# A graph layer's gather and segment sum: 56 window quads and 423 gathered chunks in place of 64 and 352, stores by SyncE, the second sort beside the first quads, the loop unrolled

## The chip, the cores and the metric

The kernel runs on one core of one Trainium2 chip. Time is the device time of one execution in microseconds. The kernel before took 15,360.9 us, the median of three runs between 15,360.42 and 15,367.33.

A core has five engines with instruction queues of their own, each worked in order: TensorE (PE), VectorE (DVE), ScalarE (ACT), GpSimd (POOL) and SyncE (SP). SP, ACT and POOL can issue DMA transfers; an indirect transfer, which takes its row numbers from a table in the on-chip memory, is issued by POOL in this kernel.

## The reference

```
h = relu(layernorm(x))                       # x: 100000 x 64, float32
local, nbr = h[dst], h[src]                  # 3.3 million edges, sorted by dst
y = concat([local, nbr - local]) @ W.T + b
s = segment_sum(y, dst, 100000); cnt = segment_sum(1, dst)
out = x + where(cnt > 0, s / max(cnt, 1), 0)
```

As the layer is linear, the kernel sums the neighbours' rows h[src] for each node first, and multiplies the mean by W once per node. The heavy part is that segment sum: 3.3 million rows, picked by src, added up by dst. For precision each float32 row of h is kept as three bfloat16 parts side by side (table h3, 194 columns), so that one-hot matmuls add it exactly enough.

## The kernel before

It has four stages: a pre-stage (layer norm, the table h3 and the own part hb), a sort of the edges of the windows, the segment sum, and a post-stage (division, the matmul with W, the residual).

The edges, in order of dst, are split in two sets, which are summed in two ways at the same time.

**Quads.** The first 2,039,808 edges make 256 windows of 7968 edges; one window's dst numbers span fewer than CH = 256 nodes. Four windows make a quad, 64 quads in all. Each window's edges are sorted by src on DVE (`sort_lane`: a merge network on keys, 128 windows at once, one per partition; two such lanes). A step of the network copies one half of a piece of keys to `tmp`, a tile in PSUM, by ACT (line 455), and takes minimum and maximum by DVE (lines 456 and 457). At its end it counts where each block of 640 nodes begins (lines 533, 588). `fill_lane` then reads the sorted keys back, 32 or 64 of each window and block, by indirect transfers of POOL (kf, line 636, 161 per lane, and kx, line 721, 64 per lane for the edges left over), and writes small tables sr_d, dt_d, et_d and xs_d to DRAM by SP. `quads` streams the whole table h3, as 157 blocks of 640 nodes, through the core once per quad: SP loads three blocks at a time (tab, line 761, three buffers), with srs (line 752) and dt (line 756); DVE makes one-hots gh and dh, two blocks at a time (lines 789 and 340); PE picks rows by gh (line 811, into gp), ACT copies them (gs, line 813), and PE adds them by dh to the quad's sums (line 819, total). A quad has 158 such block steps (NE), 79 turns of the loop. At its end ACT copies total (line 835, 4 copies), DVE adds the own counts, and POOL adds each window's sums to acc in DRAM (line 849). Some edges of a quad that fit no slot are read by two indirect transfers (rows_x, line 778).

**Chunks.** The other edges make 352 chunks of 3584. `chunks` reads every edge's row by indirect transfers of POOL, 128 rows each, 28 per chunk (nb, line 391, 9856 in all), into 6 buffers of 14. DVE makes a one-hot of 14 x 128 x 128 (hot, line 340), PE adds up in PSUM (ps, line 396), DVE folds the three parts (sums, line 407), and POOL adds the 128 sums to acc (line 366, indirect, 58 chunks; line 371, a direct add at an address read from base_r, 294 chunks).

**What sets the order.** The program is written as generators that take turns. `gathers(ns)` gives out one gather of `chunks` for each GATHER = 1250 ns that the work beside it was reckoned to take, and `took` counts each fill transfer as one such. Lane 0 is sorted first, then lane 1 with lane 0's fill beside it; then four quads (U0) with lane 1's fill, all with gathers between; then a loop of three turns (`For_i`), each with 20 quads (SB) and 98 chunks (KB). `add_later` puts off the adds of a chunk or window by 56 gathers.

```
owed += 2 * (KB * J - 1) / (SB * NE)
while owed > 0:
    next(ev, None)
    owed -= 1
```

This is the loop's own pace: KB x J = 2744 gathers are spread evenly over a turn's 20 quads. At the end of the stage a test on `odd` decides whether a slow general path (lines 932 to 985) has to run; for these inputs it doesn't.

Of the kernel before, what the change touches and what calls it, by code (L numbers as in the profile page):

```python
# [32 lines left out]
LANES = 2  # L33
SB = 20
KB = 98
U0 = 4
KG = 16
# [3 lines left out]
STEP = 1050  # L41
GAP = 8
# [19 lines left out]
PIECE = 1536  # L62
COUNTS = 1
GAIN = 2.0 ** 40
PART = 1024
# [19 lines left out]
def plan(v, e):  # L85

    wl = 1 << int(np.log2(33 * CH * 1.05))
    ew = wl - PAD
    nw = LANES * P
    chunks = -(-(e - nw * ew) // CHUNK)  # L90
    return wl, nw, max(chunks, (nw // W - U0) // SB * KB)


@with_exitstack
def gnn_preln(ctx: ExitStack, tc, x, src_w, dst_w, src_p, dst_p, src_a, dst_a, wT, b, out, V, E):
# [27 lines left out]
    SETS = NL * G  # L123
# [7 lines left out]
    PA = NCH - (SETS - U0) // SB * KB  # L131
# [4 lines left out]
    assert 2 * C == P and NCB % 2 == 1 and PA >= 0 and SL % 2 == 0  # L136
# [9 lines left out]
    wb_d = dram.tile([SETS * W, 1], I32, name="wb_d")  # L146
# [28 lines left out]
    wb_r = consts.tile([1, SETS * W], I32, name="wb_r")  # L175
    turns = consts.tile([1, 2], I32, name="turns")
    ones = consts.tile([P, 1], F32, name="ones")
# [4 lines left out]
    odd = consts.tile([P, 1 + 5 * LANES], F32, name="odd")  # L182
# [22 lines left out]
    with tc.tile_pool(name="pre", bufs=2) as pre, tc.tile_pool(name="small", bufs=4) as small, \  # L205
# [32 lines left out]
        most = small.tile([P, NMT], F32, name="most", bufs=1)  # L238
        nc.vector.memset(least, 0.0)
        nc.vector.memset(most, 0.0)  # L240

        def bounds(m):
# [3 lines left out]
            nc.vector.tensor_reduce(least[:n, m:m + 1], d[:n], axis=AX.X, op=ALU.min)  # L246
            if m == NMT - 1:

                nc.vector.scalar_tensor_tensor(d[:n], d[:n], float(V), d[:n], op0=ALU.is_lt, op1=ALU.mult)
            nc.vector.tensor_reduce(most[:n, m:m + 1], d[:n], axis=AX.X, op=ALU.max)  # L250
            if m < NMT - 1:
                return
            span = small.tile([P, NMT], F32, name="span", bufs=1)
            nc.vector.tensor_sub(span, most, least)
            nc.vector.tensor_reduce(odd[:, 0:1], span, axis=AX.X, op=ALU.max)
            nc.vector.tensor_scalar(odd[:, 0:1], odd[:, 0:1], float(P), None, op0=ALU.is_ge)
# [55 lines left out]
    with tc.tile_pool(name="rows", bufs=6) as rows, \  # L312
# [5 lines left out]
        def number(at, engine, most):  # L318
            with tc.issue_after(last[engine].ins):
                return nc.values_load(at, engines=[engine], min_val=0, max_val=most)  # L320
# [5 lines left out]
        later = []  # L326
        count = [0, 0]
# [4 lines left out]
        def add_now(all_of_them=False):  # L332
            while later and (all_of_them or (later[0][0] <= count[0] and count[0] - count[1] >= GAP)):
                later.pop(0)[1]()
                count[1] = count[0]

# [8 lines left out]
        def chunks(first, n, dynamic=None):  # L345


            def load(q):
# [7 lines left out]
                nc.vector.tensor_sub(rel[:, :k], di[:, :k], base_b[:, at][:, :, None].to_broadcast([P, k, J]))  # L356
                near = index.tile([P, KG, J, D], I16, name="near")
                nc.vector.tensor_scalar(near[:, :k], rel[:, :k, :, None].to_broadcast([P, k, J, D]), float(2 * CH), None,
                                        op0=ALU.min)
                to = index.tile([P, KG], I32, name="to", bufs=3)  # L360
                nc.vector.tensor_scalar(to[:, :k], base_b[:, at], pcol, None, op0=ALU.add)
                return si, near, to

            def addition(q, rows_to, sums):
                if dynamic is None:
                    nc.gpsimd.indirect_dma_start(  # L366
                        out=acc, out_offset=bass.IndirectOffsetOnAxis(ap=rows_to, axis=0),
                        in_=sums, in_offset=None, compute_op=ALU.add)
                else:
                    at = number(base_r[0:1, ds(dynamic + q, 1)], POOL, V)  # L370
                    nc.gpsimd.dma_start(acc[ds(at, P)], sums, accum_op=ALU.add)  # L371

            ahead = load(0)
            before = None
            parts = J // JH
            for k in range(n * parts + 1):
                q, part = divmod(k, parts)
                u = q % KG
                if q < n:
                    if u == 0 and part == 0:  # L380
                        si, near, to = ahead
                    hot = rows.tile([P, JH, P], BF16, name="hot", bufs=4)
                    nb = rows.tile([P, JH, CT], BF16, name="nb")
                    with behind():
                        one_hot(hot, near[:, u, part * JH:part * JH + JH], P)
                if before is not None and before[2] == 0:
                    ps = rows_ps.tile([P, CE], F32, name="ps")
                for j in range(JH):
# [6 lines left out]
                    if before is not None:  # L395
                        nc.tensor.matmul(ps, lhsT=before[0][:, j], rhs=before[1][:, j, :CE],  # L396
# [7 lines left out]
                if before is not None and before[2] == parts - 1:  # L404
                    sums = rows.tile([P, C1], F32, name="sums", bufs=LAG + 2)
# [4 lines left out]
                    add_later((LAG - 1) * J, lambda b=before[3], s=sums: addition(*b, s))  # L410
                if q < n:
                    before = (hot, nb, part, (q, to[:, u:u + 1]))
# [5 lines left out]
        def sort_lane(l, keys, piece, few, ps):  # L418

            whole = keys.bitcast(I32)  # L420
# [3 lines left out]
            nc.vector.tensor_scalar_min(wb[:, 0:1], wb[:, 0:1], float(V - CH))  # L424
            last[DVE] = nc.vector.tensor_reduce(wb[:, 1:2], whole[:, :EW], axis=AX.X, op=ALU.max)
# [6 lines left out]
            mine = slice(l * P, l * P + P)  # L432
            for i in range(W):
                nc.sync.dma_start(wb_d[mine].rearrange("(g i) o -> i g o", i=W)[i], wb_i[i * G:i * G + G])
            nc.sync.dma_start(wb_r[:, mine], wb_d[mine].rearrange("w o -> o w"))
            for a in range(0, EW, PART):
# [12 lines left out]
                last[DVE] = nc.vector.scalar_tensor_tensor(d, d, 1, s[:, :n],  # L449
                                               op0=ALU.logical_shift_left, op1=ALU.bitwise_or)  # L450
# [3 lines left out]
            def exchange(lo, hi, tmp):  # L454
                last[ACT] = nc.scalar.copy(tmp, lo)  # L455
                nc.vector.tensor_tensor(lo, tmp, hi, ALU.min)  # L456
                last[DVE] = nc.vector.tensor_tensor(hi, tmp, hi, ALU.max)  # L457
# [601 lines left out]
```

## Time and profile before

| what | value | where it is from |
|---|---|---|
| median of the runs | 15,360.9 us | times |
| the profiled execution | 15,353.34 us, span 15,351.7 us | times, page |
| granted TensorE clock, mean | 0.889 | profile by cores |
| first and last gather (line 391) | 437.5 and 14,998.8 us | the tile nb |
| first fill of lane 0, of lane 1 (line 636) | 1568.1 and 2594.6 us | timeline of POOL |
| first gp matmul of the quads | 2575 us | timeline |
| HBM traffic | 267 GB/s over the span, some 310 in the loop | page |

The span is what the profiler saw from the first to the last instruction; the time has 1.6 us more. The page gives for each engine its busy time, which counts neither the waits nor the sequencer's own steps. A group's row has the line, the engine, the operation, the tile written and those read, how often, then its busy time, the mean of one in ns, and the idle time just before its instructions with what ended it; "issue" there is idle time in which the engine waited for nothing that the profile shows. Rows of a table by stretches give the length, the busy time of each engine with the number of its instructions, the granted clock, the share of time in which the DMA engines were busy, and GB/s. A pause on an engine that nobody waits for costs nothing.

### The profile page before, as it was taken

The page shows a single profiled execution, that of the slowest core. Times are in us where ns is not written, and L with a number is a line of the kernel's source. Part 1 is how long each engine was busy: PE and PEld are TensorE (multiplying, and loading weights), DVE is VectorE, ACT ScalarE, POOL GpSimd, SP SyncE. Part 2 cuts the span into 40 slices and gives each one's busy share as a digit, 9 for nine tenths or more (in the row PEclk, how much of TensorE's full clock was granted, in tenths as well). Part 3 has the DMA queues.
Part 4 walks back from the last instruction along what each step waited for, and adds up shares of the span by engine and source line. Part 5 has one row for each costly group of instructions (what it writes and reads, how often), then busy time and mean ns, then how long its engine had stood idle before and what let it go on. Part 6 is the DMA issues. An engine that isn't in the chain of part 4 may idle for free. (4 is left out here: it accounts for less than half of the span.)

```text
span 15351.7 us, 559362 instructions
## 1 busy us (share of the span) xinstructions
PE 11536.5 (75%) x238778; PEld 9464.2 (62%) x238778; DVE 11308.7 (74%) x15452; ACT 6104.8 (40%) x11710; POOL 11131.2 (73%) x11210
## 2 busy tenths in 40 slices
PE   6101001596998989998799999899879999989985
PEld 5100001475777777777677777777767777777775
DVE  6889797675777777777677777777767777777774
ACT  5335344342444444444344444444334444444441
POOL 4776766547777777777777777777777777777776
PEclk7555555798999999999899999999999999999997
DMA  7573233796999999999899999999989999999997
GB/s 295 124 106 55 48 52 80 189 318 213 313 314 309 318 306 309 307 312 306 264 309 321 311 318 307 304 311 315 299 268 314 319 309 312 313 307 310 311 302 281
DMA packets 1746424, 4097.89 MB, mean 267 GB/s; under 512 B 943899, under 2 KB 952230, under 8 KB 1738950
## 3 DMA queue, kind: packets, MB, share of 16 engines
q1 hardware_dynamic: 1182534, 3461.26, 64.6%
q0 software_dynamic: 454208, 535.92, 17.0%
q10 hardware_dynamic: 107168, 64.74, 2.1%
q8 instruction: 1877, 30.75, 0.8%
q14 instruction: 637, 5.22, 0.1%
HBM read 3880.72 MB, written 219.04 MB: 267 GB/s over the span
## 5 line engine op out<-in xcount | busy, mean ns | idle before, releaser
L391 POOL DMA_INDIRECT nb<-h,si x9856 | 9427.8, 957 | 3263.5 <-issue 2820.4
L813 ACT CAST gs<-gp 128x386 bf16<-128x386 f32 x10048 | 4830.0, 482 | 7085.4 <-PE gp L811 6870.8
L811 PE MATMUL gp<-tab,gh 128*128 128x193 bf16 x60288 | 6225.4, 251 | 978.0 <-DMA tab<-tables 590.5
L811 PEld LDWEIGHTS <-gh 128*128 128x128 bf16 x60288 | 4887.1, 99 | 1992.3 <-issue 923.2
L340 DVE TENSOR_TENSOR dh<-dt,c 128x1024 bf16<-128x1024 int16 x5056 | 3454.8, 683 | 2861.1 <-PE total L819 2728.8
L789 DVE TENSOR_TENSOR gh<-srs,c 128x1536 bf16<-128x1536 int16 x5056 | 4765.1, 942 | 19.0 <-PE gp L811 17.5
L819 PE MATMUL total<-gs,dh 32*128 32x193 bf16 x160768 | 4411.6, 247 | 40.8 <-issue 38.6
L819 PEld LDWEIGHTS <-dh 32*128 32x128 bf16 x160768 | 3193.2, 94 | 1073.2 <-issue 1054.1
L396 PE MATMUL ps<-nb,hot 128*128 128x193 bf16 x9856 | 1802.3, 263 | 2458.4 <-DVE sums L409 1862.0
L396 PEld LDWEIGHTS <-hot 128*128 128x128 bf16 x9856 | 972.4, 104 | 2417.1 <-DVE sums L409 1911.8
L455 ACT COPY tmp<-keys 128x1536 f32<-128x1536 f32 (+14 forms) x540 | 650.3, 1214 | 1226.6 <-DVE keys L457 1009.1
L456 DVE TENSOR_TENSOR keys<-tmp,keys 128x1536 f32<-128x1536 f32 (+14 forms) x540 | 757.1, 1423 | 80.3 <-ACT tmp L455 79.3
L340 DVE TENSOR_TENSOR hot<-near,c 128x1792 bf16<-128x1792 int16 x704 | 760.4, 1080 | 9.6 <-PE ps L396 9.5
L457 DVE TENSOR_TENSOR keys<-tmp,keys 128x1536 f32<-128x1536 f32 (+14 forms) x540 | 757.1, 1422 | 2.3
L849 POOL DMA_DIRECT2D acc<-wsums x256 | 347.6, 1358 | 191.8 <-DVE gh L789 67.3
L636 POOL DMA_INDIRECT kf<-ksort,at_i x322 | 308.9, 959 | 98.7 <-issue 87.9
L371 POOL DMA_DIRECT2D acc<-sums x294 | 301.8, 1027 | 14.7 <-DMA acc<-wsums 7.7
L407 DVE TENSOR_REDUCE sums<-ps 128x64 f32<-128x192 f32 x352 | 123.9, 352 | 144.1 <-PE ps L396 143.8
L839 DVE SCALAR_TENSOR_TENSOR whole<-own,whole 128x193 f32<-128x193 bf16 x512 | 191.7, 417 | 35.1 <-ACT whole L835 34.3
L303 PEld LDWEIGHTS o_ps<-w_own,hT 128*128 128x128 f32 x784 | 155.5, 253 | 81.9 <-ACT hT L298 72.0
L366 POOL DMA_INDIRECT acc<-sums,to x58 | 94.8, 1635 | 150.3 <-DVE sums L409 131.1
L721 POOL DMA_INDIRECT kx<-ksort,xat x128 | 120.8, 944 | 107.3 <-DVE xat L718 53.8
(174 smaller groups left out, 3573.4 us busy)
## 6 DMA issues: line engine op xcount, KB each, us to landing
tab<-tables SPq DMA_DIRECT2D x3328, 727.5 KB
srs<-sr_d SPq DMA_DIRECT2D x1216, 512.0 KB
nb<-h,si POOLq DMA_INDIRECT x9856
tables<-h ACTq DMA_DIRECT2D x157, 242.5 KB
h<-parts SPq DMA_DIRECT2D x28, 1358.0 KB
acc<-zeros SPq DMA_DIRECT2D x28, 910.0 KB
at<-acc SPq DMA_DIRECT2D x28, 910.0 KB
xt<-in_x SPq DMA_DIRECT2D x28, 896.0 KB
```

The costliest lines, as they stand in the source:

```text
L340: nc.vector.tensor_tensor(out.rearrange("p k (a d) -> p k a d", d=D), numbers[:, :, None].to_broadcast(shape), upto[:shape[0], :n].rearran ...
L391: last[POOL] = nc.gpsimd.indirect_dma_start(out=nb[:, j], out_offset=None, in_=h3, in_offset=bass.IndirectOffsetOnAxis(ap=si[:, u, at:at + ...
L396: nc.tensor.matmul(ps, lhsT=before[0][:, j], rhs=before[1][:, j, :CE], start=before[2] == 0 and j == 0, stop=before[2] == parts - 1 and j ...
L455: last[ACT] = nc.scalar.copy(tmp, lo)
L456: nc.vector.tensor_tensor(lo, tmp, hi, ALU.min)
L457: last[DVE] = nc.vector.tensor_tensor(hi, tmp, hi, ALU.max)
L636: last[POOL] = nc.gpsimd.indirect_dma_start(out=kf[:, c], out_offset=None, in_=ksort, in_offset=bass.IndirectOffsetOnAxis(ap=at_i[:, c0 + ...
L789: nc.vector.tensor_tensor(gh[:, :m].rearrange("p c i b s -> p (c i) b s"), srs[u, s // SL][:, c:c + m].rearrange("p c i s -> p (c i) s")[: ...
L811: nc.tensor.matmul(gp[:, i], lhsT=ghots[t][:, i, b], rhs=row[:, b + i * (NB - NR), :CE], start=b == 0, stop=b == NR - 1)
L813: nc.scalar.copy(gs[t], gp)
L819: nc.tensor.matmul(total[:, i, to(b)], lhsT=hot[at, b * P:b * P + P], rhs=of[at], start=flags.get("start", False) and b == 0, stop=flags.g ...
L849: nc.gpsimd.dma_start(acc[ds(at, CH)].rearrange("(b p) c -> p b c", p=P), sums, accum_op=ALU.add)
```

## The change

- 56 quads instead of 64 (lanes of 32 and 24; a lane's sort and fill still use all 128 partitions) and 423 chunks instead of 352: 11,844 gathers instead of 9856. Lane 1's spare partitions repeat windows.
- A chunk's edges are laid out so that one gather holds 128 consecutive edges. Its dst numbers then lie near a known place, and the one-hot is made only 32 nodes wide (BAND), into four fixed tiles that are zero elsewhere; the matmul reads it shifted. The test in the pre-stage (`bounds`) checks that the edges keep to the band.
- Sums are no longer added to acc but stored, by SP. Two neighbours share at most their boundary node, so each store is followed by a copy of the next one's first row to a side table, and the next store overwrites it; the side tables are added at the end (six indirect adds). The first three chunks are kept in the on-chip memory and added last, by POOL.
- Lane 0 is sorted alone; its fill begins just ahead of the first quad; lane 1 is sorted and filled beside the first 32 quads, with pieces of at most 1024 keys and `tmp` in SBUF instead of PSUM.
- No `For_i`: all quads and chunks are unrolled. In the last 24 quads one in five of the table loads is kept in SBUF. Several buffers become fewer.

```
-LANES = 2
-SB = 20
-KB = 98
-U0 = 4
-KG = 16
+PARTS = (32, 24)
+LANES = len(PARTS)
+U1 = 32
+KG = 8
-STEP = 1050
-GAP = 8
+STEP = 3050
+BEHIND = 1.0
+BAND = 32
+GAP = 4
+EARLY = 3
+KEEP = 5
-PIECE = 1536
+PIECE = (1536, 1024)
-PART = 1024
+PART = 256
...
+            e = pre.tile([P, CHUNK], I32, name="e", bufs=1)
+            nc.vector.tensor_tensor(e[:n].rearrange("c (p j) -> c p j", j=J), d[:n].rearrange("c (p j) -> c p j", j=J),
+                                    drift_i[:n, None, :].to_broadcast([n, P, J]), ALU.subtract)
...
+            nc.vector.tensor_reduce(off[:n, 0, m:m + 1], e[:n], axis=AX.X, op=ALU.max)
...
+            nc.vector.tensor_reduce(off[:n, 1, m:m + 1], e[:n], axis=AX.X, op=ALU.min)
...
-    with tc.tile_pool(name="rows", bufs=6) as rows, \
+    with tc.tile_pool(name="rows", bufs=5) as rows, \
...
-            def addition(q, rows_to, sums):
-                if dynamic is None:
-                    nc.gpsimd.indirect_dma_start(
...
+                def put():
+                    at = number(base_r[0:1, c], SP, V)
+                    last[SP] = nc.sync.dma_start(acc[ds(at, P)], sums)
+
+                def shared():
+                    at = number(base_r[0:1, after], SP, V)
+                    last[SP] = nc.sync.dma_start(side_c[c], acc[ds(at, 1)])
+
+                add_later((LAG - 1) * J, put)
+                add_later((LAG - 1) * J + GAP, shared)
...
-                    hot = rows.tile([P, JH, P], BF16, name="hot", bufs=4)
+                    hot = narrow[part][q % 2]
...
-                        one_hot(hot, near[:, u, part * JH:part * JH + JH], P)
+                        one_hot(hot[:, part * JH * D:][:, :JH * (P + D)].rearrange("p (k x) -> p k x", x=P + D)[:, :, :BAND],
+                                near[:, u, part * JH:part * JH + JH], BAND)
...
+            def both(part, n):
+                finish = part()
+                if soft:
+                    yield 0
+                    yield 0
+                finish()
+                yield 2.083 * n + 290
...
+                if s < NCB and s % TG == 0 and kept is not None and s // TG % KEEP == 0:
+                    tabs[u, s // TG] = kept[:, s // TG // KEEP]
...
-                        at = number(wb_r[0:1, ds(w, 1)], POOL, V - CH)
-                        nc.gpsimd.dma_start(acc[ds(at, CH)].rearrange("(b p) c -> p b c", p=P), sums, accum_op=ALU.add)
...
+                def put():
+                    at = number(wb_r[0:1, w], SP, V)
+                    last[SP] = nc.sync.dma_start(acc[ds(at, CH)].rearrange("(b p) c -> p b c", p=P), sums)
...
+                    begin = fill_lane(0, fill, took)
+                    for _ in range(4 * SL):
+                        next(begin)
+                    rest = behind_quads()
+                    left = 0.0
+                    for i, _ in enumerate(quads(0, U1, late=True)):
+                        if i < NE // 2 - 10:
+                            for _ in range(4):
+                                next(begin, None)
+                            gathers(STEP / 2)
+                        else:
+                            drain(begin)
+                            left += BEHIND
+                            while left > 0:
+                                left -= 1 + next(rest, 0) / 1500
+                            gathers(STEP)
...
+                pace = (NCH * J - count[0]) / ((SETS - U1) * NE // 2 - 4)
+                owed = 0.0
+                for _ in quads(U1, SETS - U1, kept):
+                    gathers(pace * GATHER)
...
-                with tc.For_i(0, (SETS - U0) // SB, 1) as g:
-                    ev = chunks(None, KB, PA + g * KB)
...
+        for k in range(-(-SETS * W // P)):
+            add_side(k, side_w, wb_d, 0, min(P, SETS * W - k * P))
+        for k in range(NMT):
+            add_side(k, side_c, base_i.rearrange("m p -> (m p)")[:, None], 0 if k else EARLY, min(P, NCH - 1 - k * P))
```

`behind_quads` runs lane 1's `sort_lane` and `fill_lane` one after the other; `add_side` loads up to 128 side rows and their node numbers by ACT and adds them to acc by one indirect add of POOL.

## The prediction

> **What bounds the kernel now.** I began with the chain that ended last, and it says nothing: it holds only the last stage (lines 999 to 1018, some 350 us). So I went to busy time by engine, then to groups by line.
>
> ```profile
> PE 11536.5 (75%) x238778; PEld 9464.2 (62%) x238778; DVE 11308.7 (74%) x15452; ACT 6104.8 (40%) x11710; POOL 11131.2 (73%) x11210
> ...
> L391 POOL DMA_INDIRECT nb<-h,si x9856 | 9427.8, 957 | 3263.5 <-issue 2820.4 <-PE ps L396 220.7 <-DMA nb<-h,si 94.6
> L636 POOL DMA_INDIRECT kf<-ksort,at_i x322 | 308.9, 959 | 98.7 <-issue 87.9 <-DMA kf<-ksort,at_i 6.1 <-ACT gs L813 2.1
> L849 POOL DMA_DIRECT2D acc<-wsums x256 | 347.6, 1358 | 191.8 <-DVE gh L789 67.3 <-DVE dh L340 52.3 <-DMA acc<-wsums 50.8
> L371 POOL DMA_DIRECT2D acc<-sums x294 | 301.8, 1027 | 14.7 <-DMA acc<-wsums 7.7 <-DVE sums L409 6.6
> ```
>
> By busy share POOL looks loosest of the three, at 73%. But the gather's row has 2820 us of idle time put down to "issue", time in which POOL waited for nothing. The timeline of POOL in the middle of the loop shows what that is.
>
> ```profile
> 6508.36 0.94 POOL L391 DMA_INDIRECT nb<-h,si  x1 [0.30 <-issue]
> 6509.61 0.94 POOL L391 DMA_INDIRECT nb<-h,si  x1 [0.30 <-PE gp L811]
> 6510.86 0.94 POOL L391 DMA_INDIRECT nb<-h,si  x1 [0.30 <-issue]
> 6511.81 1.03 POOL L371 DMA_DIRECT2D acc<-sums  x1
> 6513.14 1.04 POOL L391 DMA_INDIRECT nb<-h,si  x1 [0.30 <-issue]
> ```
>
> Every indirect transfer has 0.30 us ahead of it, whatever went before; a direct add has none. A gather costs POOL 6509.61 − 6508.36 = **1.25 us** (median over the trace 1.249), not the 0.944 that counts as busy. The same step stands at 450.28 and 451.53, in the sort, before any loop. So I counted POOL's work anew, by stretches:
>
> ```profile
> 2575.00:3012.00 437.00, 201.99 (x3594) 164.69 (x3594) 254.62 (x565) 120.44 (x202) 275.04 (x288) 0.71 0.66 168
> 3186.00:3358.00 172.00, 160.11 (x3615) 131.35 (x3612) 133.05 (x187) 76.50 (x161) 91.11 (x93) 1.00 0.95 316
> ...
> 7700.00:11000.00 3300.00, 2991.26 (x64934) 2450.88 (x64933) 2455.11 (x3444) 1362.94 (x2848) 2511.73 (x2595) 0.98 0.95 311
> ```
>
> Columns: length, then PE, PEld, DVE, ACT, POOL busy (instructions), clock, DMA share, GB/s. From 7700 to 11000 POOL issued 2595 transfers: 2437 indirect x 1.249 + 85 x 1.03 + 72 x 1.36 (lines 371 and 849) = 3229 of 3300 us. It is full at 98%; a quad there takes about 188 us (20 quads and 2744 gathers per turn of some 3770 us). The second row is one whole quad, its 16 whole-copies of line 835 being 172 us apart, with only 93 POOL transfers beside it: 116 us of POOL. There the transfers bound it, DMA at 95%. So a quad needs 172 us of DMA and PE, and POOL makes it 188. **POOL's list of transfers is the bound**, with DMA and PE a tenth behind; only the stretch before 3600 has holes in it.
>
> **The change on POOL.** The instruction streams of both kernels give the counts. Gone: 294 + 256 + 58 adds, 301.8 + 347.6 + 94.8 = 744 us busy, and 58 x 0.30 for the indirect ones, 762 in all; three direct adds and six indirect ones come back at the very end. Gone too: 16 of 128 row loads of line 778, as there are 8 quads fewer. Added: 71 chunks x 28 = 1988 gathers. Fill transfers stay at 322 + 128 (both lanes keep 128 partitions).
> - before: (9856 + 322 + 128 + 128) x 1.249 = 13,032, plus 762: 13,794 us. The first gather starts at 437.5 and the last add of the loop's end at 14,999.7: 14,562 us, so 768 us of holes.
> - after: (11,844 + 322 + 128 + 112) x 1.249 = **15,495 us**, +1701.
> Nothing in the change makes a gather cheaper: same 128 rows of 194 values from the same table, same instruction.
>
> **What it takes from PE, DVE and DMA** (8 quads of 172 us, the wide one-hots at 1080 ns, a fifth of the table loads in the last 24 quads) costs and saves nothing, since POOL covers it: 193 gathers are programmed per quad in the first 32 (3050 / 1250 x 79), and about 228 in the last 24. That is 241 and 285 us of POOL, 2.5 more with the row loads, against 172 needed.
> - Sorting lane 1 behind the quads: one lane's exchanges are (757.1 + 757.1) / 2 = 757 us on DVE (lines 456, 457), with loads, counts and fill about 1000; over 32 quads 31 us beside the 133 of the second row above: 164 under 241. If that cover is gone it is 31 per quad.
> - Stores on SyncE: 420 chunks + 224 windows, each a store and a row copied, some 11 pairs per quad. A store must have landed before its row is read, 2.5 us by the waits at the end (below), at worst 11 x 2 x 3 = 66 us per quad of the queue. Behind them wait the table loads, three buffers of three blocks, 9 x 241 / 158 = 13.7 us ahead. Covered, at 0; uncovered, 66 per quad, still 172 + 66 under 241.
> - Gather buffers 6 to 5: 70 gathers, 87 us ahead; 0.
> - The loop gone: each turn's end shows about 17 gathers missing (128 and 130 in 200 us against 146), 20 us; the end of the first 32 quads takes such a place, so I count 20.
>
> **Where POOL will stand idle.** In the changed order 784 gathers stand ahead of lane 0's fill (161 kf, 64 kx), then six row loads, then gather 785. Its buffer is freed by PE's matmuls on group 51, and those stand in PE's stream 1.81 quads in. So:
> - Pre-stage. The new bounds test has two more passes over 3584 values and one more tile: DVE 4 x (3 x 3.88 + 4.2) + 13 = 76 instead of 28 us (3.88 is line 246's, 4.2 is line 443's 1.22 for 1024 values scaled, 13 the last tile's masks). Between 0 (hidden) and 48; taken: 25. First gather 462.
> - 784 x 1.249: POOL is through at 1441. Lane 0's fill started at 1568.1, 1131 after the first gather. Out of that stretch go lane 1's loading (two scans of 8.45, eight pieces of lines 443 to 449 at some 5.2: 59) and 56 one-hots narrowed by about 0.69 (39), less overhead of smaller pieces; bounds 0 and 98, taken 70, as DVE wasn't always busy: fill starts at 1523.
> - Lane 1's fill and the quad beside it are the model of what follows: kf 2594 to 2801 (207), kx first at 2884 and last at 2981, the quad's end at 3012. So kf to 1730, kx 1813 to 1910, quad 0 ends 1943. Then 0.81 of a quad at 172: gather 785 at **2083**.
> Up to there POOL has done 784 + 225 + 6 transfers, 1268 us of 1621: 354 us of holes against 768. Bounds: 200 (quad 1 runs beside quad 0's end) to 600 (quad 0 takes the 437 of the first row above, from a fill that starts late).
>
> **Lane 1's exchanges** now read two operands in SBUF; before, one was in PSUM. The nearest rows are the load of lane 0, with two SBUF inputs in lines 356 and 443:
>
> ```profile
> 452.78 1.42 POOL L391 DMA_INDIRECT nb<-h,si  x1 [0.30 <-issue]
> ...
> 454.05 1.22 DVE L443 TENSOR_TENSOR own<-s,keys 128x1024 int32<-128x1024 int32 x1
> 454.50 1.58 POOL L391 DMA_INDIRECT nb<-h,si  x1 [0.30 <-issue]
> ...
> 835.79 0.98 DVE L443 TENSOR_TENSOR own<-s,keys 128x800 int32<-128x800 int32 x1
> 836.63 0.95 POOL L391 DMA_INDIRECT nb<-h,si  x1 [0.30 <-issue]
> ```
>
> A gather met by line 443 took 0.95, or 1.58 where line 358's conversion ran just before. 757 / 1.249 = 606 gathers run beside the exchanges: 0 to 606 x 0.64 = 388 us. I take 26, near the lower end, as the clean row (836.63) shows nothing. The Trainium skill speaks against the change here: "SBUF — State Buffer", "Who interferes with whom", has a DVE instruction with two SBUF inputs contend with a GpSimd one that reads SBUF, one blocking the other for a whole instruction; half of a 1.22 us exchange for each of 606 gathers would make 370 us, by my estimate from that page, and the total some 345 higher. The page infers that descriptor writing escapes this.
>
> Lane 1's own fill may hold POOL up where its three buffers wait for DVE: 0 to 100, taken 30. Together 26 + 20 + 30 = 76.
>
> **The end.** The last gather to the end took 353 us. The adds there show how a chain of them runs:
>
> ```profile
> 15006.09 1.20 POOL L849 DMA_DIRECT2D acc<-wsums  x1 [2.25 <-DMA acc<-sums]
> 15009.76 1.20 POOL L849 DMA_DIRECT2D acc<-wsums  x1 [2.47 <-DMA acc<-wsums]
> ```
>
> 3.67 us each. After the last store come 3 direct and 6 indirect adds: 3 x 3.67 + 6 x 4.4 = 37, and some 10 for the row copies: 400.
>
> **Sum**: 462 + 15,495 + 354 + 76 + 400 = 16,787. The profiled span, 15,351.7, lies 9 under the median of the runs: **16,796**, 9.3% slower.
>
> **Rivals.**
> - *The holes close* (quad 0 ends as soon as its fill lands, and lane 1 disturbs nothing): 16,787 − 354 + 100 − 76 = 16,457, so about 16,470. For it: kf alone is 201 us; against: the 83 us between kf and kx are a chain on DVE that is still there. 0.10.
> - *Lane 1 gets in the way*: the quad that ran beside a fill took 437, 265 more than one without. If that returns around quads 22 to 26 with nothing of it covered, and the exchanges cost 388: 16,796 + 265 + 362 = about 17,420; half of it 17,100. For it: the fill's stores queue on SyncE with the new ones; against: each quad has 70 us of slack. 0.18.
> - *A cheaper gather, and so faster*: the 0.30 us ahead of each indirect transfer goes, because the adds on POOL or the wide one-hots caused it. 11,391 transfers follow gather 785; from (15,352 − 400 − 2083 − 76) / 11,391 = 1.123 us down the kernel is not slower, and at 0.944 it ends at 2083 + 10,753 + 476 = 13,312. Against: the step is 1.249 with and without adds near. 0.05.
> - That the change doesn't do what it says: the streams show 11,844 gathers, so only the time is open.
>
> **Numbers.** Likeliest, 0.66: 16,796, its own range 16,550 to 17,000. With the rivals on the slower side the range is 16,430 to 17,150; outside lie the cheaper gather and the worse half of lane 1. Faster 0.05, the one rival on that side; within 0.2% (31 us, about what this kernel's runs can tell from no change) 0.01; slower 0.94.
>
> **What would show it.** The step of gathers at 1.249 in every stage (wrong if 1.12 or less); POOL idle for about 170 us up to 2083 and some 80 each ahead of kf and kx; quads 244 us apart up to number 32 and 287 after, with PE near 70% and DMA well under 95%; 11,391 transfers in a row from there. Wrong in size if the kernel shows quads bound by another engine: DVE waiting on `tmp`, or table loads late behind a store.

## The result, and the profile after

The changed kernel took 17,430.1 us (median of four, 17,423.2 to 17,451.7); the kernel before, run beside it on the same chip, 15,364.1 (15,360.4 to 15,375.8). The ratio is **1.1346, 95% interval 1.1326 to 1.1365**: 2,066 us slower, where 1,435 had been predicted. The direction was right, the size too small by some 630 us, and outside the range. The profiled execution has a span of 17,450.1 us at a granted clock of 0.822; it is the slowest of the four, some 20 us over the median, so that the terms below add up to 663 us more than predicted. Two of the chips that later runs fell on ran every kernel far slower, the one before at 24,820 us; the eight runs there are set against the kernel before on the same chip and can't be read for POOL.

First the engines and the rows of the page of the changed kernel that answer to those of before: busy time and mean of one, then the idle time ahead and what ended most of it.

```profile
PE 11068.0 (63%) x212494; PEld 9053.9 (52%) x212494; DVE 10037.1 (58%) x14843; ACT 5485.9 (31%) x10639; POOL 12231.3 (70%) x12584
...
L421 POOL DMA_INDIRECT nb<-h,si x11844 | 11267.9, 951 | 4458.8 <-issue 3415.6
L872 PE MATMUL gp<-tab,gh 128*128 128x193 bf16 x48000 | 5318.2, 261 | 4551.4 <-DMA tab<-tables 3448.4
...
L500 DVE TENSOR_TENSOR keys<-tmp,keys 128x1024 f32<-128x1024 f32 (+15 forms) x609 | 773.5, 1281 | 91.2 <-ACT tmp L495 90.3
```

POOL has 11,844 gathers, and again "issue" ahead of nearly all. What is new is the end of the second row: PE's matmul gp waited 3,448 us for table loads; in the kernel before it was 590. The timeline of POOL, late in the kernel, shows the step of a gather:

```profile
11601.11 0.95 POOL L421 DMA_INDIRECT nb<-h,si  x1 [0.30 <-DMA nb<-h,si]
11602.36 0.94 POOL L421 DMA_INDIRECT nb<-h,si  x1 [0.30 <-issue]
```

11,602.36 − 11,601.11 = 1.25 us, as before. So all of POOL's time can be split as the prediction split it: 1.249 us for each indirect transfer, the time by which a gather was busy beyond 0.944 us ("lengthening"), and the rest, in which POOL stood ("holes").

| term | predicted, us | measured, us |
|---|---|---|
| first gather | 462 | 472 |
| 12,406 indirect transfers x 1.249 | 15,495 | 15,495 |
| up to gather 785: holes (and lengthening) | 354 | 431 + 13 = 444 |
| from gather 785 to 4,035 us | part of 76 | 236 + 80 = 316 |
| 4,035 to 9,865 us | part of 76 | 293 + 1 |
| 9,865 us to the last gather | part of 76 | 32 + 3 |
| last gather to the end | 400 | 394 |
| span | 16,787 | 17,450 |

Now the table by stretches of the changed kernel: length, then PE, PEld, DVE, ACT and POOL busy (instructions), clock, DMA share, GB/s. The first two rows are quads 1 and 3, the third is quad 11, the fourth one of the last 24.

```profile
1926.00:2243.00 317.00, 198.59 (x3584) 155.51 (x3584) 295.40 (x362) 140.64 (x234) 42.15 (x41) 0.84 0.53 168
...
2555.00:2864.00 309.00, 206.72 (x3728) 164.88 (x3726) 302.23 (x363) 142.16 (x239) 202.39 (x195) 0.86 0.65 197
...
5038.00:5290.00 252.00, 184.66 (x3647) 150.88 (x3651) 134.21 (x207) 76.97 (x161) 182.61 (x194) 0.87 0.75 240
11547.00:11829.00 282.00, 182.63 (x3762) 151.22 (x3760) 137.04 (x215) 76.53 (x161) 213.13 (x227) 0.83 0.64 194
```

In the first quads the bound isn't POOL: DVE is busy 302 of 309 us. In quad 11 nothing is full, and yet it takes 252 us where POOL's 194 transfers need 242. In the last 24 quads POOL is full again: 227 transfers x 1.249 = 284 us.

The waits of SyncE's own queue and of PE, from 4,262 to 9,865 us (total, times, longest):

```profile
SPq L372 <- DMA nb<-h,si: 461.2, 54, 44.0
SPq L827 <- DMA rows_x<-h,xs: 456.5, 21, 47.7
SPq L393 <- DMA acc<-sums: 212.1, 72, 6.0
SPq L920 <- DMA acc<-wsums: 184.6, 53, 6.1
...
PE gp L872 <- DMA tab<-tables: 1279.3, 364, 43.3
```

And the same wait of PE in 3,300 us of the kernel before's loop:

```profile
PE gp L811 <- DMA tab<-tables: 146.4, 179, 3.9
```

SyncE, which loads the tables, stands 918 us at loads of row numbers (lines 372 and 827) and 397 us at the copies of a row behind a store (393 and 920); in those 3,300 us of the kernel before the loads of row numbers waited 1.8 us in all, and there were no stores on SyncE. There the longest wait of PE for a table was 3.9 us; now it is 43.

### The profile page after: what moved, and what is told of

The parts are those of the page before. It is cut to its first block, busy times and chain, and to the rows that moved or that the text cites. A ratio compares the mean times of both kernels' runs of the same rounds, so it can differ in the third digit from the quotient of the medians.

```text
span 17450.1 us, 499013 instructions
## 1 busy us (share of the span) xinstructions
PE 11068.0 (63%) x212494; PEld 9053.9 (52%) x212494; DVE 10037.1 (58%) x14843; ACT 5485.9 (31%) x10639; POOL 12231.3 (70%) x12584
## 5 line engine op out<-in xcount | busy, mean ns | idle before, releaser
L421 POOL DMA_INDIRECT nb<-h,si x11844 | 11267.9, 951 | 4458.8 <-issue 3415.6
L872 PE MATMUL gp<-tab,gh 128*128 128x193 bf16 x48000 | 5318.2, 261 | 4551.4 <-DMA tab<-tables 3448.4
L846 DVE TENSOR_TENSOR gh<-srs,c 128x1536 bf16<-128x1536 int16 (+1 forms) x4424 | 4192.8, 948 | 6001.5 <-PE gp L872 5976.6
L872 PEld LDWEIGHTS <-gh 128*128 128x128 bf16 x52752 | 4540.1, 102 | 5530.4 <-issue 3276.7
L874 ACT CAST gs<-gp 128x386 bf16<-128x386 f32 x8792 | 4194.1, 482 | 9477.2 <-PE gp L872 9175.5
L880 PE MATMUL total<-gs,dh 32*128 32x193 bf16 x140672 | 4083.9, 255 | 23.3 <-issue 13.9
L360 DVE TENSOR_TENSOR dh<-dt,c 128x1024 bf16<-128x1024 int16 (+1 forms) x4424 | 2994.2, 677 | 227.6 <-PE total L880 217.8
L495 ACT COPY tmp<-keys 128x1024 f32<-128x1024 f32 (+15 forms) x609 | 671.8, 1111 | 1253.6 <-DVE keys L501 1028.7
L500 DVE TENSOR_TENSOR keys<-tmp,keys 128x1024 f32<-128x1024 f32 (+15 forms) x609 | 773.5, 1281 | 91.2 <-ACT tmp L495 90.3
L501 DVE TENSOR_TENSOR keys<-tmp,keys 128x1024 f32<-128x1024 f32 (+15 forms) x609 | 775.5, 1284 | 13.4
L872 PE MATMUL gp<-kept,gh 128*128 128x193 bf16 x4752 | 509.7, 253 | 15.4 <-DVE gh L846 15.4
```

The costliest lines, as they stand in the source:

```text
L360: nc.vector.tensor_tensor(out.rearrange("p k (a d) -> p k a d", d=D), numbers[:, :, None].to_broadcast(shape), upto[:shape[0], :n].rearran ...
L421: last[POOL] = nc.gpsimd.indirect_dma_start(out=nb[:, j], out_offset=None, in_=h3, in_offset=bass.IndirectOffsetOnAxis(ap=si[:, u, at:at + ...
L495: ins = nc.scalar.copy(tmp, lo)
L501: ends_at(nc.vector.tensor_tensor(hi, tmp, hi, ALU.max))
L846: nc.vector.tensor_tensor(gh[:, :m].rearrange("p c i b s -> p (c i) b s"), srs[u, s // SL][:, c:c + m].rearrange("p c i s -> p (c i) s")[: ...
L872: nc.tensor.matmul(gp[:, i], lhsT=ghots[t][:, i, b], rhs=row[:, b + i * (NB - NR), :CE], start=b == 0, stop=b == NR - 1)
```

## The experiments

### The parts of the change, on two slow chips

The first four kernels fell on one slow chip, four more on a second (before: 24,822 and 24,819 us). "split64" is 64 quads and 352 chunks with the rest of the change; "spread" queues each exchange of lane 1's sort behind the latest work of the quads on its engine; "early" keeps the pace of the gathers ahead of lane 0's fill from falling behind; "gap8" puts twice the distance between two stores; "all64" is the first three together.

```
-PARTS = (32, 24)                       split64
+PARTS = (32, 32)
-STEP = 3050
+STEP = 2350
...
-                ins = nc.scalar.copy(tmp, lo)              spread
+                with tie(ACT) if soft else nullcontext():
+                    ins = nc.scalar.copy(tmp, lo)
...
+                    with tie(DVE) if soft else nullcontext():
+                        nc.vector.tensor_tensor(lo, tmp, hi, ALU.min)
+                        ends_at(nc.vector.tensor_tensor(hi, tmp, hi, ALU.max))
...
+                            owed = max(owed, 0.0)          early
...
-GAP = 4                                gap8
+GAP = 8
```

`tie(ACT)` is the latest gs (line 874), `tie(DVE)` the latest one-hot dh.

> The changed kernel with its split undone: 64 quads and 352 chunks again (lanes of 32 and 32; the pace of gathers beside the first quads set to 2350 ns a turn so that they spread evenly). Theory A (POOL's list of transfers is the bound, 1.249 us each, in the new kernel as in the old): 10,434 indirect transfers instead of 12,406 take 2463 us off; the first wait for gather 785 grows from 1.84 to 2.24 quads, some 127 us: 17,450 - 2463 + 127 = 15,110, between 14,850 and 15,350, so the rest of the change gains. Rival B (the other parts, stores on SyncE, the second sort beside the quads, are what makes it slow): above 15,364. Rival C (the gathers are not the bound): within 300 us of 17,430.

> The changed kernel with lane 1's exchanges tied behind the quads' own one-hots and casts in the queues of DVE and ACT, so that the sort spreads over some 18 quads instead of 5. Theory A (DVE, filled by the sort in quads 1 to 5, starves POOL there: 230 us of holes between 2243 and 4035 and about 100 ahead of gather 785): 17,100, between 17,000 and 17,200, and quads 1 to 5 take about 245 us instead of 311. Rival B (SyncE's stores and loads hold the quads up there): 17,430 within 60, quads 1 to 5 still near 310.

> The changed kernel with gathers given out from the first turn of quad 0 on, instead of after the 225 fill transfers have been paid for; gather 785 then stands behind 0.28 quads of PE's work instead of 1.84. Theory A (POOL is the bound, so that its wait of 256 us ahead of gather 785 is worth its length): about 250 less, 17,180, between 17,120 and 17,280. Rival B (DVE's queue in quads 1 to 5 sets how far the stage is at 3500 us, so gathers earlier help nothing): over 17,350.

> The changed kernel with 8 gathers instead of 4 between a store and the copy of the next row and between one such pair and the next, so that SyncE finds each store landed. Theory A (SyncE's waits for its own stores make the table loads late, PE late, and so POOL wait for buffers: 293 us of holes from 4035 to 9865): 17,430 less 100 to 250. Rival B (the holes there have another cause, such as SyncE's waits for index and row loads): 17,430 within 40.

> The kernel of e1 once more, since there the kernel before itself took 24,822 us, with PE's matmuls 0.7 us apart for stretches in which it waited for nothing, which hides what the split costs. As for e1: theory A (POOL's transfers at 1.249 us are the bound) 15,110, between 14,850 and 15,350; rival B (stores and the second sort are what makes it slow) above 15,364; rival C (gathers not the bound) within 300 of 17,430.

> The kernel of e2 once more, for the same reason. Theory A (the sort in DVE's queue in quads 1 to 5 starves POOL) 17,100, between 17,000 and 17,200, quads 1 to 5 near 245 us; rival B (SyncE's stores and loads hold them up) 17,430 within 60, quads near 310.

> The kernel of e3 once more, for the same reason. Theory A (the wait of 256 us ahead of gather 785 is worth its length) 17,180, between 17,120 and 17,280; rival B (DVE's queue in quads 1 to 5 sets the progress, so earlier gathers help nothing) over 17,350.

> The three edits together: 64 quads and 352 chunks, lane 1's exchanges tied behind the quads' one-hots and spread over 24 quads, gathers from quad 0 on (pace 2350 ns a turn). Theory A: start 472 + 10,434 x 1.249 = 13,032 + 150 of holes around lane 0's fill + 60 ahead of gather 785 + 0 to 290 in the quads + 97 of lengthened gathers + 394 at the end: 14,400, between 14,200 and 14,550, faster than the kernel before. Rival: at 185 us of POOL per quad the quads' own need (172 by DMA, 133 + 40 on DVE) is no longer covered, and stalls of SyncE cost what POOL had hidden: 14,800 or more.

| kernel | first chip: us, ratio (interval) | second chip: us, ratio (interval) |
|---|---|---|
| split64 | 25,956, 1.0455 (1.0438 to 1.0473) | 25,930, 1.0451 (1.0434 to 1.0469) |
| spread | 26,988, 1.0873 (1.0855 to 1.0891) | 26,959, 1.0860 (1.0842 to 1.0878) |
| early | 27,013, 1.0885 (1.0867 to 1.0903) | 26,993, 1.0876 (1.0858 to 1.0894) |
| gap8 | 27,171, 1.0948 (1.0929 to 1.0966) | |
| all64 | | 25,463, 1.0261 (1.0244 to 1.0278) |

None of these ratios tells the theories apart, and the reason is in the timeline of PE of the kernel gap8:

```profile
8058.48 0.32 PE L880 MATMUL total<-gs,dh 32*128 32x193 bf16 x1 [1.08 <-issue]
8059.92 0.33 PE L880 MATMUL total<-gs,dh 32*128 32x193 bf16 x1 [1.12 <-issue]
```

One matmul in 1.4 us, waiting for nothing that the profile shows: 5,605 us of such idle time ahead of the matmul total, 4,207 ahead of gp. POOL stood 10,094 us until PE's matmul ps had read its buffers. PE is the bound here, and POOL's terms are covered. Of these kernels split64, spread and all64 were measured on other chips too, as the next sections show; early and gap8 were not, so what they gain by themselves is open.

### 64 quads with the rest of the change

> The kernel of e1 and e5 once more, for a chip on which the kernel before takes its 15,360 us. Theory A (POOL's transfers at 1.249 us each are the bound): 15,110, between 14,850 and 15,350. Rival B (stores and the second sort make it slow): above 15,364. Rival C (gathers not the bound): within 300 of 17,430. Where PE crawls as in e1 and e5, all three fail together: near 25,900.

16,182.8 us against 15,362.3, ratio 1.0535 (1.0505 to 1.0566). The rival held. The new division of the edges, with the pace set for it, is worth 17,430 − 16,183 = 1,247 us of the 2,066; **the rest of the change, which takes 762 us of adds off POOL, makes the kernel 820 us slower**. By POOL's terms, against before: transfers and adds −762; holes and lengthening 2,284 instead of 768; the first gather 26 later; the end 68 longer: together +848, the difference of the spans (16,199.3 − 15,351.7). One stretch of its segment sum, in the columns used above:

```profile
10000.00:14000.00 4000.00, 3359.01 (x71903) 2784.44 (x71903) 2611.52 (x3911) 1503.03 (x3138) 2873.37 (x3042) 0.93 0.78 248
```

The kernel before had PE at 2,991 of 3,300 us (91%) and DMA at 0.95 there; here it is 84% and 0.78, and a quad takes about 205 us instead of 188. Nothing is full.

### Lane 1's sort spread over the quads

> 56 quads as in the changed kernel; the only edit: each exchange of lane 1's sort is queued behind the latest quad's own work on ScalarE and VectorE, so that the sort is spread over the quads. Theory (the crowding of lane 1's sort into quads 1 to 5 is the cost that the prediction left out): the holes of POOL between gather 785 and 4035 us (308 and 230 us, less the 50 or so that spread work would have left) and the 76 us by which gathers lengthened there shrink together by 250 to 400 us, and nothing comes in their place: ratio to the kernel before 1.105 to 1.120, that is 16,980 to 17,210 us. Rival (the quads are bound by SyncE's queue, and sorting early only cost what it would cost anywhere): the holes move to the quads between 2,200 and 9,900 us in which the sort now stands, and the ratio stays at 1.128 to 1.140, that is 17,330 to 17,520 us.

17,293.5 us against 15,347.9, ratio 1.1266 (1.1248 to 1.1285): between the two. First the min of lane 1's exchanges alone (line 500) by quads, in the changed kernel: DVE's busy time and number.

```profile
1926.00:2243.00 317.00, 83.84 (x73) 0.84 0.53 168
2243.00:2555.00 312.00, 88.19 (x78) 0.90 0.65 196
...
2864.00:3177.00 313.00, 90.53 (x76) 0.85 0.63 195
```

Then the same instruction (line 507 there) in the run with the sort spread:

```profile
2369.00:2629.00 260.00, 20.09 (x18) 0.86 0.74 235
...
6776.00:7042.00 266.00, 20.37 (x17) 0.86 0.75 238
```

And its whole stretches, all engines: a quad with the sort beside it, and the one in which lane 1's fill now falls.

```profile
2629.00:2893.00 264.00, 187.74 (x3749) 153.44 (x3741) 171.49 (x242) 93.72 (x180) 199.33 (x202) 0.85 0.73 233
7042.00:7537.00 495.00, 223.07 (x3727) 181.03 (x3726) 267.06 (x601) 172.45 (x368) 337.76 (x348) 0.71 0.56 157
```

As the program is written, an exchange takes 4.6 of a quad's 79 turns (three steps of 1, and 2,423 / 1,500), that is 17 a quad. Lane 1 has 339 exchanges, so at that pace they fill 20 quads, and not the 32 that I had counted on; the run with the sort spread keeps to it. In the changed kernel as built there are 73 to 78 a quad. With the crowding undone, gather 785 comes at 2,078.7 us instead of 2,184.6, and the quads behind it take 260 instead of 310. But not all of it is won: spread over more gathers, the exchanges lengthen them by some 165 us up to 7,150 us (80 in the changed kernel up to 4,035). Lane 1's fill makes one quad 495 us long, but most of that is POOL's own work, 347 transfers at 1.249, and only 52 us are holes. By the medians crowding costs 137 us net, not the 250 to 400 that I expected.

### 64 quads, the sort spread, the pace kept

> The kernel of e8 once more (64 quads and 352 chunks, lane 1's exchanges tied behind the quads' one-hots, gathers from quad 0 on). e9 showed, beside POOL's list, quads of 205 us where the kernel before has 185, with PE waiting for table loads and SyncE waiting for its own row copies and stores. Theory D (POOL's waits in e9 before 4200 us, 413 ahead of gather 785 and 452 beside the sort, go, but SyncE keeps quads near 205): 16,183 less 350 and 300, 15,500, between 15,350 and 15,700, quads after the sort at 200 to 210. Theory A (only POOL and the sort count): 14,400 to 14,600, quads at 185. Rival (the sort, spread, costs each quad what it saves): 15,900 or more.

15,860.4 us against 15,400.8, ratio 1.0301 (1.0271 to 1.0331): between theory D and the rival. Spreading the sort and keeping the pace are together worth 323 us here (16,183 − 15,860), though gather 785 comes 614 us earlier (1,689 us instead of 2,303); quads still took about 198 us behind the sort, and POOL stood 298 of the 4,000 us from 10,000 on.

### Without the row copies, and with stores from ScalarE

> The changed kernel with 56 quads, its stores kept on SyncE, but the copies of one boundary row behind each store and the final adds of those rows are left out (the rows shared by two neighbours come out incomplete). Theory (SyncE's queue makes the table loads late, because a store has to land before the row behind it is read): the 290 us of POOL's holes between 4,035 and 9,865 us fall to under 130, the wait of matmul gp for tab there from 1,279 to under 900 us, the tail by some 25 us: ratio to the kernel before 1.113 to 1.124, 17,100 to 17,270 us. Rival (the row loads and index loads in SyncE's queue, whose buffers come free late, are the cause, or the quads are bound elsewhere): the holes stay over 200 us, ratio 1.126 to 1.135.

> The changed kernel with 56 quads; the stores and the row copies are issued from ScalarE's queue instead of SyncE's, nothing else. Theory (SyncE's queue): table loads are never behind a store; holes between 4,035 and 9,865 us under 150 of 290; but ScalarE, 31% busy, now waits 2.5 to 5 us for each landing, 22 times a quad, so that its copies gs come late in places: ratio 1.110 to 1.128. Rival (the landing waits cost wherever they stand, as ScalarE stands in every block step): ratio over 1.135, with matmul gp and total waiting for gs.

```
-                add_later((LAG - 1) * J + GAP, shared)     e12, also for windows
...
-                    at = number(base_r[0:1, c], SP, V)     e13, and so for all four
-                    last[SP] = nc.sync.dma_start(acc[ds(at, P)], sums)
+                    at = number(base_r[0:1, c], ACT, V)
+                    last[ACT] = nc.scalar.dma_start(acc[ds(at, P)], sums)
```

Without the copies: 17,315.0 against 15,360.6, ratio 1.1276 (1.1258 to 1.1295). The holes from 4,035 to 9,865 us fell from 293 to 200, and the end from 394 to 357 (the adds left out). The wait of PE didn't fall (waits of SyncE and PE, the same stretch):

```profile
SPq L372 <- DMA nb<-h,si: 631.4, 51, 59.6
SPq L826 <- DMA rows_x<-h,xs: 571.4, 21, 61.8
...
PE gp L871 <- DMA tab<-tables: 1338.8, 288, 56.8
```

SyncE stands 285 us longer at the row numbers (1,203 us instead of 918), most of the 397 that it no longer stands at the copies. So the copies are a third of that stretch's loss, and the rival held for the rest.

With stores and copies from ScalarE: 17,832.8, ratio 1.1613 (1.1593 to 1.1632). Waits of ScalarE and PE there:

```profile
ACT gs L874 <- DMA side_c<-acc: 837.7, 115, 18.6
ACT gs L874 <- DMA side_w<-acc: 316.1, 54, 16.6
...
PE gp L872 <- ACT gs L874: 936.9, 229, 15.9
```

gs stands behind the store and its copy for up to 18.6 us, and PE behind gs. POOL's holes from 4,035 to 9,865 us rose to 490. The rival held, and the landing wait costs more on an engine that has work in every block step. PE's wait for tables fell to 397 us, as the theory had it; it is another wait that took its place.

### 64 quads with stores from ScalarE, and with third buffers

> 64 quads and 352 chunks, lane 1's sort spread behind the quads' own work, pace never behind, three buffers instead of two for the index and row loads, stores and row copies from ScalarE's queue. All else of the change stays (narrow one-hots, stores in place of adds, no loop). Theory (SyncE's queue is what made quads take 198 us in place of some 185): quads fall to 182 to 190 us, holes after 8,400 us to under 250, and the kernel comes to 15,000 to 15,400 us, ratio 0.975 to 1.003. Rival (the quads are bound by the DMA engines and PE beside the sort, SyncE only shows it): ratio 1.015 to 1.035, as without these two edits (1.030).

17,235.5 us, ratio 1.1225 (1.1206 to 1.1244): worse than either theory allowed, by the same wait of gs (566 us at the chunks' copies from 10,000 to 14,000 us).

> The changed kernel with 56 quads and a third buffer for si (the row numbers of eight chunks' gathers) and for xs, et and rows_x (a quad's row loads); nothing else. Theory (what makes table loads late is that SyncE's queue stands up to 50 us at the load of si or xs, whose buffer POOL has not read yet; the row copies only add to it): the 917 us that SyncE waits for nb and rows_x between 4,262 and 9,865 us fall under 200, matmul gp's wait for tab there from 1,279 to under 600 us, POOL's holes between 4,035 and 9,865 us from 293 to under 100, and the ratio comes to 1.112 to 1.124 (17,085 to 17,265 us). Rival (SyncE waits there only because POOL is full, and what it loads then is early enough): gp's wait for tab moves by less than 200 us and the ratio stays at 1.128 to 1.137.

> 64 quads and 352 chunks, lane 1's sort spread behind the quads' own work, pace never behind, a third buffer for the index and row loads; stores and row copies on SyncE as in the change. Theory (the waits of SyncE for nb and rows_x cost some 300 us of holes after 8,400 us in that version without the third buffers, which took 15,860 us): holes between 10,000 and 14,000 us fall from 298 to under 150, ratio 1.005 to 1.020. Rival (the row copies, or a bound in DMA and PE): holes there stay over 220, ratio 1.024 to 1.034.

```
-                si = index.tile([P, KG, J], I32, name="si")
+                si = index.tile([P, KG, J], I32, name="si", bufs=3)
...
-                    xs = load.tile([P, NX], I32, name="xs", bufs=2)
+                    xs = load.tile([P, NX], I32, name="xs", bufs=3)
```

(et and rows_x alike; with 64 quads all tiles of the index pool.) With 56 quads: 17,425.1 us, ratio 1.1346 (1.1327 to 1.1365), the same as without, and gp waited 1,298 us for tables instead of 1,279: the rival's figures. The waits of SyncE:

```profile
SPq L372 <- DMA nb<-h,si: 475.1, 53, 43.0
...
SPq L827 <- DMA rows_x<-h,xs: 431.4, 19, 50.3
```

With 64 quads: 15,751.0 us, ratio 1.0257 (1.0240 to 1.0274), where the rival put it; holes from 10,000 to 14,000 us 287 instead of 298. It is the best version found, and slower than the kernel before; its interval and that of the version without the third buffers (1.0271 to 1.0331) overlap. Its larger loss lies beside the sort: from 2,400 to 6,900 us POOL stood 528 of 4,500 us, with quads of 210 to 233 us whose 150 transfers need 187, and PE waited 704 us for tables there. Two other parts of the change, the five gather buffers for six and the loop unrolled, were undone in no run.

The trace shows why a buffer more doesn't shorten these waits. Counted over eight loads of si between 7,000 and 9,500 us, SyncE issues one when the first gather that reads it is 7.9 to 8.0 chunks away, one load's worth; with three buffers 15.9 to 16.0 chunks, two loads' worth. Each time that is just when its buffer is read out. In the same stretch xs follows the end of a pair of rows_x by 3 to 4 us; in the kernel before, from 7,700 to 11,000 us, it came 87 to 125 us behind one. So the load was put in SyncE's queue at the place where its buffer comes free, however many there are. SyncE runs ahead of POOL, and there it stands until POOL has come. The timeline of SyncE in the changed kernel (start, length):

```profile
7234.27 7.29 SPq L818 DMA_DIRECT2D tab<-tables  x2
7264.20 0.40 SPq L372 DMA_DIRECT2D si<-in_src_p  x1
7264.71 0.51 SPq L818 DMA_DIRECT2D tab<-tables  x1
...
```

and PE after it:

```profile
7269.58 1.15 PE L872 MATMUL gp<-tab,gh 128*128 128x193 bf16 x6 [17.21 <-DMA tab<-tables]
```

SyncE issued nothing from 7,241.6 to 7,264.2; PE went on 5 us after the table load behind was issued, and had waited 17 us. Of PE's waits for tables from 4,262 to 9,865 us, 32 were longer than 8 us, 708 us together, and every one ended within 12 us of SyncE's leaving such a load. That is an association in the trace, not an experiment: a kernel with these loads put back to where the program calls them wasn't tried, nor one with KG back at 16, which would halve the loads of si.

A wait of PE isn't yet a hole of POOL. Two stretches of the changed kernel, quads 9 to 20 and quads 22 to 26:

```profile
4523.00:7562.00 3039.00, 2205.99 (x44722) 1801.40 (x44720) 1626.16 (x2486) 924.04 (x1932) 2238.95 (x2372) 0.87 0.76 242
7775.00:8897.00 1122.00, 888.30 (x18413) 725.12 (x18411) 669.81 (x1004) 384.83 (x806) 721.09 (x765) 0.91 0.81 262
```

In the first, PE waited 760 us for tables, and POOL was nearly full all the same: 2,371 transfers x 1.249 = 2,961 of 3,039 us. In the second, PE waited 207 us, and POOL stood 167 us, more than half of the 293 between 4,035 and 9,865. It had 139 to 173 transfers a quad there, some 205 fewer in the five quads than at 194 each. By the program `took` leaves out one gather for each of lane 1's 225 fill transfers. As built the fill runs in quads 5 and 6, but the gather stream has its gap in quads 22 to 26. Three of these quads, with 148 to 153 transfers (191 us at most at 1.249), took 214 to 220 us, where the kernel before needed 172 with 93. This too is read from the trace; no run moves the gap back.

## Why the prediction was wrong in size, by its own steps

**What bounds the kernel: right in the last 24 quads; the gather's price: right in every stage.** 1.249 us and 15,495 us of transfers, the clock at 0.82 without effect on it, and the last 24 quads at 290 us on average (predicted 287) with 32 us of holes in 7,192. The rival of a cheaper gather is dead: with the adds gone, the 0.30 us stayed.

**Up to gather 785: right in its parts, 102 us late at the end.** kf began at 1,485 (1,523 predicted), ended at 1,692 (1,730), kx ran from 1,778 to 1,859 (1,813 to 1,910), quad 0 ended at 1,926 (1,943). Then "0.81 of a quad at 172" failed: lane 1's exchanges filled DVE in quad 1, and gather 785 came at 2,184.6 instead of 2,083. With the sort spread it came at 2,078.7.

**The failed step: "over 32 quads 31 us beside the 133 of the second row above: 164 under 241."** I took the sort's pace from the program's loop, and not from the order of instructions as built, which has 73 to 78 exchanges in a quad instead of 17. (By the program's pace, too, it would have been 20 quads and not 32.) DVE then had 295 to 304 us of work in quads of 309 to 317. With the fill in quads 5 and 6 (403 and 455 us) that is 316 us in place of most of the 76; undoing it gained 0.0080 of the time before by the ratios (123 us), 137 by the medians, 173 by the spans of the two profiles.

**"Covered, at 0", of the stores on SyncE: wrong by 93 us that a run shows, in a stretch with 293 us of holes.** The bound that I wrote was 66 us of the queue per quad; the copies and stores took some 21 (212 + 185 + 88 us over 23 quads), but they, with the loads of row numbers in the same queue, left no 13.7 us ahead. A third of the 293, 93 us, is the copies (run without them). For the other 200 the trace points to two things that I had not costed at all: the place of si and xs in the queue, where SyncE stands up to 48 us, over three times the lead of the table buffers, and the gap in the gathers in quads 22 to 26. There POOL no longer covered the quad, and the "172 needed", taken from the kernel before, was 214 us or more. How the 200 us divide between them stays open.

**The exchanges' contention with gathers: 26 taken, 80 measured** (some 165 where the sort is spread), inside the bounds of 0 and 388. The clean row was no test: line 443 ran there from 835.79 to 836.77 us and the gather began at 836.63, so the two met for 0.14 us. In quads 1 to 5 of the changed kernel the 650 gathers that overlapped an exchange took 1.05 us on average, up to 2.06, and the 150 that didn't took 0.948; with the sort spread it was 1.13 (863 gathers) and 0.945. The Trainium skill ("SBUF — State Buffer", "Who interferes with whom") has such an instruction contend with a GpSimd one that reads SBUF, over ports that it calls an exclusive lock, by which I had estimated 370. The runs lie between a fifth and a half of that, so the page's sign is right, but half of the gathers that met an exchange in the changed kernel took 0.947 us or less. Whether a gather is held up in reading its row numbers or in writing its descriptors, which the page infers escapes, these runs don't separate.

**The end: right**, 394 for 400. **The rivals**: "lane 1 gets in the way" gave 17,420, and 17,430 was measured, but that agreement is luck: it had the fill uncovered (265) and 388 of contention, where 82 us of holes in the quads of the fill and 80 of contention were measured; the rest was DVE crowded in quads 1 to 4 and the later holes.

## What to carry to other kernels

Where a scheduler orders the instructions, the pace written in a loop is not the order in the queues: count, in the built stream, how many of the moved instructions stand between two of the work they are to hide behind. Work that is moved leaves a gap where it was paid for. A load that was placed as early as its buffer allowed made its queue meet the reader of that buffer; a third buffer moved the meeting and didn't remove it. Before such a wait is blamed, see whether the bound engine stands there too. And taking work off the bound engine was worth nothing while the stages that feed it weren't kept as full: with the edges divided as before, 762 us came off POOL, and 1,516 came back as holes and lengthened gathers.

## What the hardware showed that was not expected

- A small copy that needs a store's row was issued 5.1 us behind the store beside the table loads (store at 7,023.15, copy at 7,028.29); at the kernel's quiet end the same pair stood 1.5 to 1.9 us apart.
- On two chips PE issued single matmuls 0.7 or 1.4 us apart in long stretches with nothing to wait for, at granted clocks of 0.69 to 0.73 (0.81 to 0.89 on the others), and the kernel before took 24,820 us instead of 15,360. Every kernel was slower there, the one before too, and its cause stays open.
